# First weight pair of a sandwich block's gate and up products: fewer x splits beside it, down weights a pair later, the exponentials' tile kept

## The chip, the cores and the metric

The kernel runs on one core of a Trainium2 chip. The metric is the device time of one execution in microseconds, as the median of several runs. A profile of one execution shows each engine's instructions: TensorE (PE, with its weight loads PEld), VectorE (DVE), ScalarE (ACT), GpSimd (POOL), and the SP queue, which only issues DMAs here.

## What is computed

The input x has 2048 tokens of 1024 channels, everything in float32. The block is an attention part and a feed-forward part, each between two layer norms, each added to its input:

```python
def attn(x, Wqkv, bqkv, Wo, bo):
    qkv = x @ Wqkv + bqkv                        # one head, d = 256
    q, k, v = split(qkv)
    a = softmax(q @ k.T / sqrt(d))
    return (a @ v) @ Wo + bo
def ffn(x, W_gate, W_up, W_down):                # F = 2752
    return (silu(x @ W_gate.T) * (x @ W_up.T)) @ W_down.T
x = x + layernorm(attn(layernorm(x), Wqkv, bqkv, Wo, bo))
x = x + layernorm(ffn(layernorm(x), W_gate, W_up, W_down))
```

## The kernel before

**Products.** TensorE multiplies float32 numbers rounded to a shorter form (float32r). To keep precision each operand is kept as a high part and a low part, hi = round(a) and lo = a - hi. ScalarE makes the high part (a cast, L109 or L407), VectorE the low part (a subtraction, L110 or L408). One product of two blocks is then three matmuls, hi·hi, hi·lo and lo·hi (`mm3`, L144, and `mmc`, L602).

**Attention** goes by blocks of 128 queries, i = 0 to 15 (loop at L899). For a block the program computes scores (L244), the softmax into the tile `p_s` of 128 x 2048 (L253), four groups of transpositions of `p_s` that give the pieces of `pT` (`turn`, L263), the product with v (`attend`, L272: L276 and L277), the transposition of its result (`turn_o`, L282, with the copy L279 and the sum L280 before it) and the output projection (`proj`, L288). For the first 8 blocks the residual follows at once (`residual`, L299, and `xpose`, L342, which writes the transposed normalized rows to the DRAM tensors `xT_d`). For the last 8 blocks the projection only stores its rows in `at_d` (L297), and their residuals are done later, beside the gate and up products.

**Gate and up products** take two passes of 1024 tokens (s = 0, 1). In a pass there are 10 pairs of weight blocks (`gate_up`, L623). A pair multiplies 2 x 2 blocks by a scheme of Winograd's kind: seven products per weight matrix instead of eight, over sums of weight blocks (A11, A12, S1 to S4, A22) and sums of token blocks (B11, B21, B22, T1 to T4). Their order is A11·B11, A12·B21, S2·T2, S1·T1, S3·T3, A22·T4, S4·B22, each for gate and for up. With three matmuls for each of four blocks of channels, a product takes 12 matmuls of 128 x 512 (`prod`, L609, all of them on line L605). The four PSUM banks of a pass hold ag, au, cg and cu. ScalarE copies ag and au out (L637, L639 after A11·B11; L652, L654 after S2·T2; L661, L665 after S3·T3), VectorE adds (L618), ScalarE applies silu (L621), and the seven results are stored in `hd` (L634). The results lie in eight tiles `tmp` of 512 columns, which are halves of four tiles `xi`.

**The splits of x.** B11 and B21 lie in `xb`, T1 and T3 in `kx`, T2 in `qa` and `qb`, T4 and B22 in `a1`. During attention these tiles hold k, q and v, so the sums for the first pass are made early, stored in DRAM (`xs_d`, L417 and L418), and read back and split when a tile comes free. A `First` (L420) has a load into a float32 tile (L429) and a use (L407 and L408). They come in the list `order` (L939): the first four are loaded beside attention and used in its last round (L918); 4 to 9 are loaded and used from L946 on and in the first pair's jobs (`first`, `ahead`, `behind`).

**Beside a pair** of the first pass run three jobs, called from `background` (L629): after the A11 products, after the A12 products and after the S1 products. `ahead(p)` transposes the residual block of the pair before (`xpose`, L347 and L349), loads the attention rows and x of block 8 + p (L979, L980) and makes the sums of down weights of pair p (`down_weights`, L741: L744, three L618 and the four stores L749). `behind(p)` loads the next pair's down weights (`load_down`, L737) and does the residual of block 8 + p.

**Weights.** A feeder (L456) loads weight blocks (L511) and makes their sums (L529 to L532) and hi and lo parts whenever one of six slots is free; the slots are quarters of `a2` and halves of `wvo`, which attention uses until its end.

**Order on the engines.** A scheduler decides where an instruction stands in its engine's queue, by a model of time and the dependences between tiles. What is wrapped in `pin` (tc.keep_in_program_order) stays in the order of the program. Each queue then runs in order.

**Lines to follow:** `proj` L288 to L297, the tiles at L320 to L328, `tmp` in L626 and L698, the end of attention L943 to L958, the jobs L960 to L987, the loop over the pairs L989 to L996.

Of the kernel before, what the change touches and what calls it, by code (L numbers as in the profile page):

```python
# [8 lines left out]
F32 = mybir.dt.float32  # L9
# [6 lines left out]
P = 128  # L16
T = 2048
# [17 lines left out]
def block_kernel(ctx, tc, x, wqk, wv, bqk, bv, wo, bo, wgu, wlast, wd, out):  # L35
# [14 lines left out]
    def pool(name, side=None, **kw):  # L50
        return tc.alloc_tile_pool(name=name, bufs=1, side=side, reuse_waits="tile", **kw)

    def tl(p, shape, dt, name):
        return p.tile(shape, dt, tag=name, name=name, bufs=1)
# [231 lines left out]
        split(oTs[i % 2][:, :, 0, :], oTs[i % 2][:, :, 1, :], b.rearrange("p (d q) -> p d q", d=2))  # L286

    def proj(i):  # L288
        a = pair[i % 3][0] if i < EARLY else f4[i % 2]
        oT = oTs[i % 2]  # L290
        for h, b in ((1, bank[5]), (0, bank[7])):
            cols = slice(h * 512, h * 512 + 512)
            for d in range(2):
                mm3(b, (oT[:, d, 0, :], oT[:, d, 1, :]), (wo_s[:, d, 0, cols], wo_s[:, d, 1, cols]), d == 0, d == 1)
            nc.vector.scalar_tensor_tensor(a[:, cols], b, ys[i % 4][:, 13:14], bo_s[:, cols], ALU.mult, ALU.add)
        if i >= EARLY:
            nc.sync.dma_start(at_d[i], a)  # L297
# [22 lines left out]
    wpool = pool("w")  # L320
    wr = [tl(wpool, [P, C], F32, f"wr{i}") for i in range(2)]
    qb = tl(wpool, [P, 2, 2, 512], F32R, "qb")
    spool = pool("s")
    p_s = tl(spool, [P, T], F32, "p_s")
    oTs = [tl(spool, [P, 2, 2, P], F32R, f"oTs{i}") for i in range(2)]
    xe = tl(spool, [P, C], F32, "xe")
    xpool = pool("xb", side="right")
# [14 lines left out]
    def xpose(t, a, b, banks):  # L342
        for hf in range(2):
            o = banks[hf]
            for j in range(4):
                cb = 4 * hf + j
                nc.tensor.transpose(o[:, j * P : (j + 1) * P], a[:, cb * P : (cb + 1) * P], ident)  # L347
            s = b[:, hf * 512 : hf * 512 + 512]
            nc.scalar.copy(s, o)  # L349
            d = xT_d[t // TB][hf * 512 : hf * 512 + 512, (t % TB) * P : (t % TB + 1) * P]  # L350
            nc.sync.dma_start(d.rearrange("(j p) t -> p j t", p=P), s.rearrange("p (j t) -> p j t", j=4))
# [271 lines left out]
    def gate_up(s, p, wg, wu, bg, jobs):  # L623

        ag, au, cg, cu = bg
        g11, g12, g22, g21, u11, u12, u22 = tmp[0:7]  # L626
        job = list(jobs)

        def background():  # L629
            if job:  # L630
                job.pop(0)()

        def put(name, t):
            nc.sync.dma_start(hd[s][p][name], t)  # L634

        prod(ag, wg, "A11", "B11")
        nc.scalar.copy(g11, ag)  # L637
        prod(au, wu, "A11", "B11")
        nc.scalar.copy(u11, au)  # L639
        background()  # L640
        prod(cg, wg, "A12", "B21")
        wg.slot[0].done()
        add(g11, cg, g11)
        silu(g11, g11)
        prod(cu, wu, "A12", "B21")
        wu.slot[0].done()
        add(u11, cu, u11)
        add(g11, g11, u11, ALU.mult)
        put("A11", g11)
        background()  # L650
        prod(ag, wg, "S2", "T2", False)
        nc.scalar.copy(g12, ag)  # L652
        prod(au, wu, "S2", "T2", False)
        nc.scalar.copy(u12, au)  # L654
        prod(cg, wg, "S1", "T1")
        wg.slot[1].done()
        prod(cu, wu, "S1", "T1")
        wu.slot[1].done()
        background()
        prod(ag, wg, "S3", "T3", False)  # L660
        nc.scalar.copy(g22, ag)  # L661
        add(g22, cg, g22)
        silu(g22, g22)
        prod(au, wu, "S3", "T3", False)
        nc.scalar.copy(u22, au)  # L665
        add(u22, cu, u22)
        add(g22, g22, u22, ALU.mult)
        put("A22", g22)
        background()
        prod(ag, wg, "A22", "T4", False)  # L670
        wg.slot[3].done()
        silu(g21, ag)
        prod(au, wu, "A22", "T4", False)
        wu.slot[3].done()
        add(g21, au, g21, ALU.mult)
        put("A12", g21)
        prod(cg, wg, "S4", "B22", False)
        wg.slot[2].done()
        add(g12, cg, g12)
        silu(g12, g12)  # L680
        prod(cu, wu, "S4", "B22", False)
        wu.slot[2].done()
        add(u12, cu, u12)
        add(g12, g12, u12, ALU.mult)
        add(u22, g12, g22)
        add(u12, g11, g12, ALU.subtract)
        add(u11, u22, g11, ALU.subtract)
        add(g12, g21, u11, ALU.subtract)
        put("S1", u22)
        put("S3", u12)  # L690
        put("S2", u11)
        put("S4", g12)

    def gate_up_rest(s, wp, wu, bg):


        ap, au, cp, cu = bg
        g11, g12, g22, g21, u11, u12, u22 = tmp[0:7]  # L698
        prod(ap, wp, "A11", "B11")
        nc.scalar.copy(g11, ap)  # L700
        prod(au, wu, "A11", "B11")
        nc.scalar.copy(u12, au)
        prod(cp, wp, "A12", "B21")
        wp.slot[0].done()
        add(g11, cp, g11)
        silu(g11, g11)
        prod(cu, wu, "A11", "T1")
        prod(ap, wp, "S2", "T2", False)
        nc.scalar.copy(g12, ap)
        prod(au, wu, "A12", "B21", False)  # L710
        add(g11, au, g11, ALU.mult)
        nc.sync.dma_start(hr_d[s][0], g11)
        prod(cp, wp, "S1", "T1")
        wp.slot[1].done()
        prod(cu, wu, "A12", "B22", False)
        wu.one.done()
        add(u12, cu, u12)
        prod(ap, wp, "S3", "T3", False)
        nc.scalar.copy(g22, ap)
        add(u22[:FR, :], cp[FR : 2 * FR, :], g22[FR : 2 * FR, :])  # L720
        add(g22[:FR, :], cp[:FR, :], g22[:FR, :])
        silu(g22[:FR, :], g22[:FR, :])
        add(g22[:FR, :], g22[:FR, :], u22[:FR, :], ALU.mult)
        nc.sync.dma_start(hl_d[s][1], g22[:FR, :])
        prod(ap, wp, "A22", "T4", False)
        wp.slot[3].done()
        silu(g21[:FR, :], ap[:FR, :])
        add(g21[:FR, :], ap[FR : 2 * FR, :], g21[:FR, :], ALU.mult)
        nc.sync.dma_start(hl_d[s][0], g21[:FR, :])
        prod(cp, wp, "S4", "B22", False)  # L730
        wp.slot[2].done()
        add(g12, cp, g12)
        silu(g12, g12)
        add(g12, g12, u12, ALU.mult)
        nc.sync.dma_start(hr_d[s][1], g12)
# [206 lines left out]
                f.load(r)  # L942
    turn_o(NT - 1)  # L943
    proj(NT - 1)

    last = f4[2], f4[3], wr[1], bo_s  # L946
    for n in range(4, 8):
        order[n].load(last[n % 4])
    spool.release()
    xipool = pool("xi")  # L950
    xi = [tl(xipool, [P, C], F32, f"xi{i}") for i in range(4)]
    y = f4[0:4] + xi
    tmp = [xi[i // 2][:, (i % 2) * 512 : (i % 2) * 512 + 512] for i in range(8)]
    for n in range(2, 4):
# [2 lines left out]
        slots.free(flat(wvo[:, 2 * n : 2 * n + 2, :, :]))  # L957
    feed.pump()  # L958

    def late(p):  # L960
        return EARLY + p if 0 <= p < NT - EARLY else None

    def first(p):
        if p == 0:
            for n in range(4, 6):
                order[n].use()
                order[n + 4].load(last[n % 4])

    def ahead(p):

        if p == 0:
            for n in range(6, 10):
                order[n].use()
            raws2.free(wr[1])
            raws2.free(bo_s)
        if late(p - 1):
            xpose(late(p - 1), *f4[2:4], Y[0:2])
        if late(p):
            nc.sync.dma_start(f4[2], at_d[late(p)])  # L979
            nc.sync.dma_start(f4[3], x[late(p) * P : (late(p) + 1) * P, :])  # L980
        down_weights(p)

    def behind(p):
        if p + 1 < NPAIR:
            load_down(p + 1)
        if late(p):
            residual(late(p), *f4[2:4])  # L987

    load_down(0)  # L989
    for s in range(2):  # L990
        pairs, rest, dn = half[s]
        bg, other = (X, Y) if s == 0 else (Y, X)
        for p in range(NPAIR):
            jobs = [] if s else [lambda: first(p), lambda: ahead(p), lambda: behind(p)]
            gate_up(s, p, *pairs[p], bg, jobs)
        gate_up_rest(s, *rest, bg)  # L996

        def next_x(cb):
            r1, r2 = raws2.get(), raws2.get()
            build_x(2, cb, r1, r2)  # L1000
            raws2.free(r1)
            raws2.free(r2)

        if s == 0:
            run_down(s, dn, other, bg, 2 * TB * [None], [lambda cb=cb: next_x(cb) for cb in range(4)])
        else:
            xpool.release()
            x1pool = pool("x1", side="right")
            x1 = [tl(x1pool, [P, C], F32, f"x1_{k}") for k in range(2 * TB)]
            run_down(s, dn, other, bg, x1, [lambda k=k: nc.sync.dma_start(x1[k], x1_d[2 * TB + k]) for k in range(2 * TB)])  # L1010
# [39 lines left out]
```

## Time and profile before

| what | value |
|---|---|
| median of 3 runs (lowest, highest) | 1701.09 us (1698.03, 1702.44) |
| the profiled execution: its time, its span | 1700.9 us, 1699.1 us |
| mean granted TensorE clock | 0.996 |
| ScalarE, VectorE busy | 694.8 us (41%), 1100.3 us (65%) |
| chain that ended last: TensorE, VectorE, DMA | 92%, 4%, 2% |
| TensorE busy from 400 to 450 us | 46.68 us |
| TensorE busy from 450 to 500 us | 44.78 us |
| TensorE busy from 1100 to 1150 us | 48.67 us |

Times are in microseconds from the start of the span. A line of a timeline has the start, the duration, the engine, the line of the program, the operation with its output and input, and in brackets how long the engine sat idle before it and what ended that. The names of the tiles have lost their numbers, so `f` stands for f4[0] to f4[4] and f2_4. Matmuls overlap each other, so a matmul is drawn longer than the time by which it delays the next.

The chain of waits passes through the end of attention (about 437 us) into the first pair and the second one, which begins with its A11 products at 476.19 us.

### The profile page before, as it was taken

What the parts mean: (1) busy time and instruction counts of PE and PEld (TensorE: products, weight loads), DVE (VectorE), ACT (ScalarE), POOL (GpSimd) and SP (SyncE); (2) the same over time, 40 slices, a digit from 0 to 9 for tenths busy, and PEclk for the clock granted to TensorE, in tenths of its full rate; (3) what the DMA queues carried; (4) which work ended last, traced back from release to release, by engine and by line L of the source; (5) the groups of instructions that cost most, each with busy time, mean ns of one, the idle gap of its engine ahead of it and who ended that gap; (6) DMA issues with size and microseconds to landing.
All of it is one profiled execution on the core that took longest, in us unless ns stands there. A gap on an engine that the chain in (4) does not pass through costs nothing.

```text
span 1699.1 us, 21099 instructions
## 1 busy us (share of the span) xinstructions
PE 1669.2 (98%) x7764; PEld 1385.5 (82%) x7764; DVE 1100.3 (65%) x1682; ACT 694.8 (41%) x1039; POOL 91.3 (5%) x118
## 2 busy tenths in 40 slices
PE   8999999999899999999999999999999999999997
PEld 6888887888678888888888888788888888888886
DVE  8643667667787777776578457866555665455458
ACT  3222445544544444443365444433333333344343
POOL 1000000000011211110000000100000000000001
PEclk9999999999999999999999999999999999999999
DMA  6221123334676566665367666633332223566654
GB/s 214 81 81 38 38 75 121 101 118 169 218 243 209 200 215 212 217 220 183 122 204 252 215 191 198 210 106 113 130 111 100 93 94 124 209 221 192 195 189 158
DMA packets 131014, 271.00 MB, mean 159 GB/s; under 512 B 13280, under 2 KB 29792, under 8 KB 130912
## 3 DMA queue, kind: packets, MB, share of 16 engines
q1 hardware_dynamic: 128176, 262.72, 46.5%
q10 hardware_dynamic: 2736, 6.95, 1.2%
q8 instruction: 60, 0.98, 0.2%
q14 instruction: 42, 0.34, 0.1%
HBM read 185.73 MB, written 83.89 MB: 159 GB/s over the span
## 4 chain that ended last, share of the span: by engine, by line
PE 92%; DVE 4%; DMA 2%; ACT 1%; issue 1%; POOL 0%; SPq 0%; POOLq 0%; DVEq 0%; ACTq 0%
PE bank L605 69%; PE bank L146 4%; PE bank L147 4%; PE bank L148 4%; PE bank L276 3%; PE bank L277 2%; PE bank L206 2%; PE bank L268 1%; PE bank L207 1%; PE bank L347 1%; PE bank L139 1%; DVE a L110 1%; DVE small L116 0%; DMA f<-xT_d 0%; DVE wvo L110 0%
## 5 line engine op out<-in xcount | busy, mean ns | idle before, releaser
L605 PE MATMUL bank<-a 128*128 128x512 f32 x1164 | 274.2, 389 | 0.0
L605 PEld LDWEIGHTS bank<-a 128*128 128x128 f32 x1164 | 218.5, 188 | 45.3
L605 PE MATMUL bank<-xb,a 128*128 128x512 f32 x912 | 212.3, 389 | 0.1
L605 PEld LDWEIGHTS bank<-xb,a 128*128 128x128 f32 x912 | 171.1, 188 | 36.0 <-ACT xi L621 0.6
L618 DVE TENSOR_TENSOR xi<-bank,xi 128x512 f32<-128x512 f32 (+1 forms) x170 | 114.0, 682 | 115.0 <-PE bank L605 70.1
L110 DVE TENSOR_TENSOR a<-f2p,a 128x1024 fp32r<-128x1024 f32 (+2 forms) x133 | 134.6, 1012 | 58.0 <-ACT a L109 54.0
L109 ACT CAST a<-f2p 128x1024 fp32r<-128x1024 f32 (+2 forms) x133 | 117.5, 884 | 131.7 <-PE bank L605 107.2
L110 DVE TENSOR_TENSOR a<-f,a 128x1024 fp32r<-128x1024 f32 (+2 forms) x91 | 89.9, 988 | 106.5 <-ACT a L109 99.8
L605 PE MATMUL bank<-wvo 128*128 128x512 f32 x612 | 149.6, 389 | 0.0
L605 PE MATMUL bank<-kx,a 128*128 128x512 f32 x612 | 146.2, 389 | 0.0
L605 PE MATMUL bank<-a,a 128*128 128x512 f32 x588 | 140.2, 390 | 3.8 <-ACT xi L661 2.6
L605 PEld LDWEIGHTS bank<-kx,a 128*128 128x128 f32 x612 | 114.9, 188 | 23.8
L605 PEld LDWEIGHTS bank<-wvo 128*128 128x128 f32 x612 | 114.9, 188 | 23.9
L605 PEld LDWEIGHTS bank<-a,a 128*128 128x128 f32 x588 | 110.2, 188 | 27.5 <-ACT xi L661 3.0
L109 ACT CAST a<-f 128x1024 fp32r<-128x1024 f32 (+2 forms) x91 | 69.5, 764 | 141.6 <-PE bank L605 110.3
L605 PE MATMUL bank<-a,wvo 128*128 128x512 f32 x444 | 106.3, 389 | 0.0
L605 PE MATMUL bank<-kx,wvo 128*128 128x512 f32 x420 | 100.1, 389 | 0.0
L605 PEld LDWEIGHTS bank<-a,wvo 128*128 128x128 f32 x444 | 83.3, 188 | 17.3
L276 PE MATMUL bank<-a,a 128*128 128x512 f32 x256 | 94.6, 403 | 2.8 <-ACT f L349 2.0
L110 DVE TENSOR_TENSOR wvo<-f,wvo 128x1024 fp32r<-128x1024 f32 (+1 forms) x52 | 60.8, 1169 | 54.9 <-ACT wvo L109 53.8
L605 PEld LDWEIGHTS bank<-kx,wvo 128*128 128x128 f32 x420 | 78.8, 188 | 16.4
L618 DVE TENSOR_TENSOR xi<-xi,xi 128x512 f32<-128x512 f32 (+1 forms) x124 | 85.3, 688 | 5.6 <-ACT xi L621 1.5
(233 smaller groups left out, 2677.5 us busy)
## 6 DMA issues: line engine op xcount, KB each, us to landing
f2p<-wgu SPq DMA_DIRECT2D x41, 512.0 KB, 5.6
hd_S<-xi SPq DMA_DIRECT2D x80, 256.0 KB, 4.4
f<-x SPq DMA_DIRECT2D x30, 512.0 KB, 3.8
hd_A<-xi SPq DMA_DIRECT2D x60, 256.0 KB, 2.0
f<-wgu SPq DMA_DIRECT2D x22, 512.0 KB, 3.5
wr<-wgu SPq DMA_DIRECT2D x21, 512.0 KB, 5.9
f<-wd SPq DMA_DIRECT2D x20, 512.0 KB, 5.0
td_T<-f SPq DMA_DIRECT2D x40, 256.0 KB, 4.6
```

Of the source, the lines that this page charges most:

```text
L109: nc.scalar.copy(hi, src)
L110: (lo_engine or nc.vector).tensor_tensor(lo, src, f32(hi), ALU.subtract)
L139: nc.tensor.transpose(b[:, j * P : (j + 1) * P], t[:, cb * P : (cb + 1) * P], ident)
L146: nc.tensor.matmul(o, w[0], m[0], start=first, stop=False)
L147: nc.tensor.matmul(o, w[0], m[1], start=False, stop=False)
L148: nc.tensor.matmul(o, w[1], m[0], start=False, stop=last)
L206: nc.tensor.matmul(b, xg[:, c, 0, cols], wv_s[:, c, :, :].rearrange("p a f -> p (a f)"), start=(c == 0), stop=False)
L207: nc.tensor.matmul(b[:, D:], xg[:, c, 1, cols], wv_s[:, c, 0, :], start=False, stop=(c == 7))
L276: nc.tensor.matmul(b, p[:, k, 0, :], vt[:, k, :, :].rearrange("p h d -> p (h d)"), start=(k == 0), stop=False)
L277: nc.tensor.matmul(b[:, D:], p[:, k, 1, :], vt[:, k, 0, :], start=False, stop=(k == NKB - 1))
L605: one = nc.tensor.matmul(o, w[i], m[j], start=first and n == 0, stop=last and n == 2, skip_group_check=chained)
L618: nc.vector.tensor_tensor(o, a, b, op)
```

## The change

Five things change.

- The exponentials' tile `p_s` is kept: it is allocated in the pool `w`, not in `s`, which is released after attention. Its two halves become xi[0] and xi[1]. The results of a pair are named in another order over `tmp`, so that g11 and u11 lie in the first half of `p_s`, g12 and u12 in the second, g22 and u22 in xi[2] and g21 in xi[3].
- `proj` of the last block, 15, writes to `xe` and not to f4[1].
- The six x splits that remain at the end of attention (order 4 to 9) get six tiles to be loaded into in one go: f4[2], f4[3], wr[1], f4[1], f4[0], bo_s. Before, four were loaded, and two more after the first two had been used.
- In the first pair, `ahead` uses splits 4 and 5 and is called first, and `behind` uses 6 to 9.
- The residual blocks 8 to 15 come a pair later (block 8 + p - 1 beside pair p), and so do the down weights: `behind(p)` loads those of pair p, `ahead(p + 1)` makes their sums, and those of the last pair are made in a fourth job of the last pair.

```diff
     def proj(i):
-        a = pair[i % 3][0] if i < EARLY else f4[i % 2]
+        a = pair[i % 3][0] if i < EARLY else f4[i % 2] if i < NT - 1 else xe
...
     qb = tl(wpool, [P, 2, 2, 512], F32R, "qb")
+    p_s = tl(wpool, [P, T], F32, "p_s")
     spool = pool("s")
-    p_s = tl(spool, [P, T], F32, "p_s")
...
-        g11, g12, g22, g21, u11, u12, u22 = tmp[0:7]
+        g11, u11, g12, u12, g22, u22, g21 = tmp[0:7]
...
-    last = f4[2], f4[3], wr[1], bo_s
-    for n in range(4, 8):
-        order[n].load(last[n % 4])
+    last = f4[2], f4[3], wr[1], f4[1], f4[0], bo_s
+    for n in range(4, 10):
+        order[n].load(last[n - 4])
     spool.release()
     xipool = pool("xi")
-    xi = [tl(xipool, [P, C], F32, f"xi{i}") for i in range(4)]
+    xi = [p_s[:, 0:C], p_s[:, C:]] + [tl(xipool, [P, C], F32, f"xi{i}") for i in range(2)]
...
     def late(p):
-        return EARLY + p if 0 <= p < NT - EARLY else None
-
-    def first(p):
+        return EARLY + p - 1 if 1 <= p <= NT - EARLY else None
+
+    def ahead(p):
         if p == 0:
             for n in range(4, 6):
                 order[n].use()
-                order[n + 4].load(last[n % 4])
-
-    def ahead(p):
-
+            return
+        if late(p - 1):
+            xpose(late(p - 1), *f4[2:4], Y[0:2])
+        if late(p):
+            nc.sync.dma_start(f4[2], at_d[late(p)])
+            nc.sync.dma_start(f4[3], x[late(p) * P : (late(p) + 1) * P, :])
+        down_weights(p - 1)
+
+    def behind(p):
         if p == 0:
             for n in range(6, 10):
                 order[n].use()
             raws2.free(wr[1])
             raws2.free(bo_s)
-        if late(p - 1):
-            xpose(late(p - 1), *f4[2:4], Y[0:2])
-        if late(p):
-            nc.sync.dma_start(f4[2], at_d[late(p)])
-            nc.sync.dma_start(f4[3], x[late(p) * P : (late(p) + 1) * P, :])
-        down_weights(p)
-
-    def behind(p):
-        if p + 1 < NPAIR:
-            load_down(p + 1)
+        load_down(p)
         if late(p):
             residual(late(p), *f4[2:4])
 
-    load_down(0)
...
-            jobs = [] if s else [lambda: first(p), lambda: ahead(p), lambda: behind(p)]
+            jobs = [] if s else [lambda: None, lambda: ahead(p), lambda: behind(p)]
+            if s == 0 and p == 0:
+                jobs = [lambda: ahead(0), lambda: None, lambda: behind(0)]
+            if s == 0 and p == NPAIR - 1:
+                jobs.append(lambda: down_weights(NPAIR - 1))
```

More of the change, by code (lines that the diff above doesn't have):

```diff
@@ L697, in gate_up_rest @@
         ap, au, cp, cu = bg
-        g11, g12, g22, g21, u11, u12, u22 = tmp[0:7]
+        g11, u11, g12, u12, g22, u22, g21 = tmp[0:7]
         prod(ap, wp, "A11", "B11")
```

## The prediction

> **What bounds the kernel now.** I read the page's busy shares first, then TensorE's waits, then the timelines of TensorE, ScalarE and VectorE round the place that the change touches.
>
> ```profile
> PE 1669.2 (98%) x7764; PEld 1385.5 (82%) x7764; DVE 1100.3 (65%) x1682; ACT 694.8 (41%) x1039; POOL 91.3 (5%) x118
> ```
>
> TensorE (PE) is busy for 98% of the span, so an edit off TensorE can only win back idle time of TensorE. TensorE's waits, summed by who ended them (us in total, times, longest), show where that is:
>
> ```profile
> PE bank L605 <- ACT xi L637: 3.1, 2, 1.6
> PE bank L605 <- ACT xi L661: 2.6, 1, 2.6
> PE bank L285 <- DVE f L280: 1.3, 1, 1.3
> PE bank L605 <- ACT xi L639: 1.0, 1, 1.0
> ```
>
> All four belong to the first two weight pairs. TensorE's timeline (start, us, instruction, idle before it) puts them between 440 and 497 us:
>
> ```profile
> 440.31 0.44 PE L285 MATMUL bank<-ident,f 128*128 128x128 f32 x2 [1.32 <-DVE f L280]
> 441.21 0.50 PE L146 MATMUL bank<-wvo,oTs 128*128 128x512 f32 x1 [0.46 <-ACT oTs L109]
> 445.93 2.12 PE L605 MATMUL bank<-qa,a 128*128 128x512 f32 x8 [1.46 <-ACT xi L637]
> 465.17 5.74 PE L605 MATMUL bank<-a,a 128*128 128x512 f32 x24 [2.62 <-ACT xi L661]
> 470.75 5.60 PE L605 MATMUL bank<-a,wvo 128*128 128x512 f32 x24
> 476.19 11.04 PE L605 MATMUL bank<-xb,a 128*128 128x512 f32 x48
> 488.83 1.66 PE L605 MATMUL bank<-qa,a 128*128 128x512 f32 x6 [1.60 <-ACT xi L637]
> 494.43 1.03 PE L347 MATMUL bank<-ident,f 128*128 128x128 f32 x8
> 496.47 1.66 PE L605 MATMUL bank<-qa,a 128*128 128x512 f32 x6 [1.00 <-ACT xi L639]
> ```
>
> The six gaps sum to 1.32 + 0.46 + 1.46 + 2.62 + 1.60 + 1.00 = 8.46 us. A stream of matmuls costs 0.227 us each (470.75 to 476.19 is 24 of them), while a lone one is drawn 0.39 us long, so each gap costs 0.16 us more than it shows: 8.46 + 6 x 0.16 = 9.4 us, the ceiling of any gain here. From 500 to 1100 us, the table by 50 us has TensorE busy throughout.
>
> Why the gaps are there is in the queues of ScalarE and VectorE:
>
> ```profile
> 433.70 0.59 ACT L109 CAST a<-bank 128x512 fp32r<-128x512 f32 x1 [0.91 <-PE bank L268]
> 437.63 1.05 ACT L407 CAST a<-wr 128x1024 fp32r<-128x1024 f32 x1 [2.21 <-PE bank L277]
> 444.79 0.61 ACT L109 CAST a<-f 128x512 fp32r<-128x512 f32 x1
> 445.30 0.58 ACT L637 COPY xi<-bank 128x512 f32<-128x512 f32 x1
> 462.29 1.05 ACT L407 CAST a<-f 128x1024 fp32r<-128x1024 f32 x1 [3.56 <-DMA f<-xT_d]
> 464.54 0.58 ACT L661 COPY xi<-bank 128x512 f32<-128x512 f32 x1
> 446.75 0.68 DVE L110 TENSOR_TENSOR a<-f,a 128x512 fp32r<-128x512 f32 x1
> 450.38 1.22 DVE L408 TENSOR_TENSOR qb<-f,qb 128x1024 fp32r<-128x1024 f32 x1
> ```
>
> ScalarE takes its queue in order. The cast at 437.63 waits for the last attention matmul and holds up the copy behind the 1.32 us. L637 stands behind two weight casts (1.46). L661 stands behind casts of x splits still in flight (2.62).
>
> [...] at 98%, weight loads are busy 82%; I count gaps only. [...] the gaps end at evacuations (L637, L639, L661). [...] SP does so: it stores to `xs_d` at 424.09 and reads back at 427.19, after 2.7 us of waiting. [...]
>
> **The change part by part.** The built program's order tells what moves; durations are the trace's. Instruction counts hardly change (one VectorE instruction fewer), so no busy time is saved.
>
> 1. *Results in the exponentials' tile.* The first pair's result tiles g11 and u11 now lie in quarters of `p_s` already read. So L637, L639 and the table load move ahead of the last attention tile, and 20 products S1·T1 (L605 on kx) become free to run early: 2 inside attention(15), 18 between proj(14) and the transposition L285. 18 x 0.227 = 4.1 us cover the 1.32 gap (the chain L279, L280 takes about 1.7 us). Gone: 1.32 + 0.16 = 1.48. L637's gap goes too: 1.46 + 0.16 = 1.62. The 0.46 stays.
>
> New waits. (a) ScalarE now casts kx<-wr, kx<-xe, qb<-f, kx<-f ahead of the cast a<-bank on which attention(15) waits (433.70 before; TensorE reaches its matmul at 436.21, so there were 2 us of slack). L637, L639, table load and silu fill it to 431.6; the four casts take 0.96 each, but the last waits for data. The two loads of an x split into f4[1] now stand ahead on SP, so the write that wr's reload waits for ends about 1.4 us later (512 KB at some 370 GB/s), and the last of the six loads is issued near 430.3 instead of 429.5. Before, it took 5.9 us and landed at 435.4. Bounds: 434.8 (bytes over the rates seen) and 435.9 (before's spacing, shifted); I take 435.4. Then cast 435.4 to 436.4, a<-bank to 437.0: TensorE loses 0.78, and 0.27 more for the next weight cast (S1): 1.05. If the cover is gone, each us of lateness is a us. (b) The S2·T2 products lose their cover, the 20 kx products. Call T0 the end of L285 (440.76 before, about 445.0 after). VectorE's queue from there is full as before: the low parts of wvo, of the second S2 weight (446.75 before), then wvo again, then qb (450.38 before, now without the two L618 in front). They end at T0 + 6.68, + 7.74 and + 8.95. TensorE reaches the second S2 product's low part at T0 + 5.60 and waits 1.08; it reaches qb's low part at + 7.80 and waits 1.15. Bounds: 0 (were VectorE early) and 2.6. I take 2.23. Sum of part 1: -1.48 - 1.62 + 1.05 + 2.23 = +0.18 us. The early copies by themselves win nothing.
>
> 2. *The last x splits at once.* f4[1] and f4[0] are free since proj(15) writes to xe and the down weights come later, so all four a1 splits have landed when ScalarE reaches them (before: landing 7.7 us after issue, at 463.5). ScalarE can start them only after the copy L654 and two weight casts, near 458.9; four at 0.96 end at 462.7, and L661 at 463.3. TensorE ends S3·T3 at T0 + 17.6 = 462.7, 0.60 earlier. 2.62 + 0.16 falls to 0.60: -2.18. VectorE's low parts follow at 1.14 each, just ahead of TensorE, since the products are now ordered by block; the add before S4·B22 has only 0.2 us of slack. Bounds of what remains: 0 and 1.5.
>
> 3. *Down weights and residual out of the first pair.* L744, three L618, the statistics of L116 to L120: about 5.3 us of VectorE between 465 and 490, with ScalarE's L303 and L308 (1.2 each) and SP's at_d, td and x1_d transfers, go to the second pair and later. The last of it runs at the end of the tenth pair, where VectorE is 51% busy (800 to 850 us) and TensorE has work queued; if that cover were gone, 5 us of VectorE would show once. The second pair's L637 waited for VectorE's last L618 at 487.48. Now g11's last reader ends near 481.6 and the products reach bank 0 near 485: hidden with 3 us to spare. -1.60 - 0.16 = -1.76.
>
> 4. *No transposition beside the second pair.* L347 (8 matmuls) stood before L639's copy; ScalarE took it and L349 first. In the third pair and on, L639 precedes L349, and the trace shows no wait there. -1.00 - 0.16 = -1.16; the 8 transposes only move to the tenth pair. SP's loads of the second pair's weights move by a few us either way and are wanted more than 5 us after they land: no cost.
>
> Sum: 0.18 - 2.18 - 1.76 - 1.16 = -4.92 us. The profiled execution took 1700.9 us (span 1699.1); 1700.9 - 4.9 = 1696.0. The median of the runs shown is 1701.09, 0.2 above it, so 1696.1 us.
>
> **Rivals.**
> - *VectorE is early (greater gain).* If (b) falls away or the loads land at 434.8, the gain is 6 to 7.5 us: 1694. For it: VectorE has slack before 440. Against: from T0 its queue runs back to back.
> - *The late kx load takes it.* Loads land at 438 (the 7.7 us seen for the later ones): 2.6 us more of stall, 1698.9. For it: ScalarE's queue is in order, with attention behind. Against: fewer bytes are in flight at 430.
> - *The change does little but reorder*: that is part 1 as I work it out, and it would be the whole only if 2 and 3 failed: 1700 to 1701.
> - *Slower: the store of S2 becomes the bound in every pair.* L639 of each pair waits for the S2 store of the pair before (24.2 us of ScalarE waiting in eight pairs), and ends 1.9 us (third pair) or more before TensorE wants its bank. Should stores land over 1.9 us later with results packed in one tile, each of 17 pairs pays: 0.6 us beyond the point makes 17 x 0.6 = 10 us, 1706.3. Against: the order of stores on SP stays the same in every pair.
>
> **How the numbers follow.** Forecast 1696.1, own range 1694.3 to 1698.3: 0.58. Greater gain, 1692.5 to 1694.3: 0.20. Late load or little gain, 1698.3 to 1701: 0.15. Slower: 0.07. A change of under 0.3% (5.1 us) is about what a measurement of this kernel can't tell from none; that bound, 1696.0, cuts the forecast in two. Faster: 0.20 + 0.34 = 0.54; same: 0.24 + 0.15 = 0.39; slower 0.07. The range that leaves out 2 in 10 is 1692.8 to 1699.6.
>
> **What would show it.** Right: no gap before L285; S2·T2 with gaps of about 1 us ended by VectorE; the gap before A22·T4 under 1 us; none before the second pair's qa products; attention(15) waiting near 436 for ScalarE. Wrong: a gap over 2 us near 436, gaps in pairs 2 and on ended by L639, or a new gap before S4·B22.

## The result and the profile after

The changed kernel takes 1695.7 us in the median of twelve runs (1695.3 to 1698.5). The kernel before, run beside it, takes 1699.56 (1697.95 to 1703.6). The ratio is 0.9977, with a 95% interval of 0.9968 to 0.9986: 3.9 us faster (2.4 to 5.4). On a second chip it came to 0.9986 (0.9980 to 0.9993), 1696.3 us and 2.4 us faster. So the forecast of 1696.1 us holds. The forecast gain of 4.9 us does not quite: the kernel before ran 1.5 us faster beside it than the 1701.09 on which the sum was built. Both gains lie under the bound of 0.3%.

On the page, TensorE is busy for as many microseconds as before, in a shorter span (1693.5 us, the execution itself 1695.4 us):

```profile
PE 1669.1 (99%) x7764; PEld 1385.6 (82%) x7764; DVE 1098.7 (65%) x1682; ACT 695.1 (41%) x1039; POOL 91.2 (5%) x118
```

TensorE's timeline from 430 to 505 us has five gaps in place of six:

```profile
437.68 0.51 PE L276 MATMUL bank<-a,a 128*128 128x512 f32 x1 [1.39 <-ACT a L109]
446.31 0.50 PE L146 MATMUL bank<-wvo,oTs 128*128 128x512 f32 x1 [0.46 <-ACT oTs L109]
452.54 1.19 PE L605 MATMUL bank<-qa,a 128*128 128x512 f32 x4 [0.98 <-DVE a L110]
454.81 2.56 PE L605 MATMUL bank<-qb,a 128*128 128x512 f32 x10 [0.84 <-DVE qb L408]
464.66 5.73 PE L605 MATMUL bank<-a,a 128*128 128x512 f32 x24 [0.94 <-ACT xi L661]
```

The gaps before L285 and of the first L637 are gone, and so are both gaps of the second pair. In their place stand the waits that the prediction named: 1.39 us ahead of attention(15), and 0.98 and 0.84 us in S2·T2. L661's gap is down from 2.62 to 0.94. The sum of the gaps falls from 8.46 to 4.61.

ScalarE's timeline shows what ends them:

```profile
434.75 1.05 ACT L407 CAST qb<-f 128x1024 fp32r<-128x1024 f32 x1
436.10 1.05 ACT L407 CAST kx<-f 128x1024 fp32r<-128x1024 f32 x1 [0.29 <-DMA f<-xs_d]
437.05 0.58 ACT L109 CAST a<-bank 128x512 fp32r<-128x512 f32 x1
...
463.08 1.04 ACT L407 CAST a<-bo_s 128x1024 fp32r<-128x1024 f32 x1
464.03 0.57 ACT L661 COPY xi<-bank 128x512 f32<-128x512 f32 x1
```

The cast of the last exponentials (437.05) stands behind a cast that waits for its load (436.10). L661 follows the casts of a1 at once; none of these waits for data any more.

**One execution is not enough here.** There are three profiles of each kernel. Three things vary between executions of the same program: how late the last x splits land, whether TensorE's granted clock falls to 0.50 for 3.4 us (below), and how long the start of the second pass takes. Stage A runs from TensorE's transposition L285 at 424.4 us to the kx,wvo products of the tenth pair (near 810), stage C from the next such products (near 1083) to the first qa,wvo products of the second pass (near 1115). The 272.0 to 272.5 us between them, and the rest after C, hardly change.

| kernel, profile | A, us | of it lost to a halved clock | L661's gap | C, us |
|---|---|---|---|---|
| before, 1 | 388.53 | - | 2.62 | 33.70 |
| before, 2 | 386.07 | - | 0.92 | 33.62 |
| before, 3 | 389.48 | 1.6 | 2.15 | 31.73 |
| changed, 1 | 384.72 | - | 0.94 | 32.04 |
| changed, 2 | 385.61 | - | 1.74 | 31.74 |
| changed, 3 | 386.09 | 1.6 | 0.46 | 33.53 |

In the means, A falls by 2.6 us (388.03 to 385.47). That is the change. C takes either about 31.9 or about 33.6 us with either kernel, so it belongs to the execution. Where it is long, TensorE waits 1.2 us for L665's copy, and on SP's queue a store (`out<-wr`, near 1071 us) is followed by the reload of its tile after 5.6 to 5.8 us, where C is short after 4.9 to 5.0 (SP's timeline, three profiles each). That the slower store makes L665 late is not shown, and why it is slower in some executions stays open. The first pair of profiles, taken alone, would have credited the change with 1.7 us of that.

### The profile page after: what moved, and what is told of

Its sections match the earlier page's. It is cut to its first block, busy times and chain, and to the rows that moved or that the text cites. A ratio compares the mean times of both kernels' runs of the same rounds, so it can differ in the third digit from the quotient of the medians.

```text
span 1693.5 us, 21093 instructions
## 1 busy us (share of the span) xinstructions
PE 1669.1 (99%) x7764; PEld 1385.6 (82%) x7764; DVE 1098.7 (65%) x1682; ACT 695.1 (41%) x1039; POOL 91.2 (5%) x118
## 4 chain that ended last, share of the span: by engine, by line
PE 94%; DVE 2%; issue 1%; DMA 1%; ACT 1%; POOL 0%; POOLq 0%; DVEq 0%; SPq 0%; ACTq 0%
PE bank L605 71%; PE bank L147 4%; PE bank L146 4%; PE bank L148 4%; PE bank L276 3%; PE bank L277 2%; PE bank L206 2%; PE bank L268 1%; PE bank L207 1%; PE bank L347 1%; PE bank L139 1%; DVE small L116 1%; PE bank L784 0%; PE bank L785 0%; DMA f<-x 0%
## 5 line engine op out<-in xcount | busy, mean ns | idle before, releaser
L618 DVE TENSOR_TENSOR p_s<-bank,p_s 128x512 f32<-128x512 f32 x96 | 65.1, 682 | 78.4 <-PE bank L605 43.2
L121 POOL TENSOR_TENSOR small<-small,mhalf 128x1 f32<-128x1 f32 x48 | 38.0, 792 | 702.6 <-DVE small L120 670.7
```

What stands on the lines that cost most here:

```text
L121: nc.gpsimd.tensor_tensor(s[:, 15:16], s[:, 14:15], mhalf, ALU.pow)
L618: nc.vector.tensor_tensor(o, a, b, op)
```

## The experiments

Each ratio is to runs of the kernel before on the same chip.

**Part 1 alone.** The kernel before with the results in the exponentials' tile:

```diff
+    p_s = tl(wpool, [P, T], F32, "p_s")
     spool = pool("s")
-    p_s = tl(spool, [P, T], F32, "p_s")
...
-        g11, g12, g22, g21, u11, u12, u22 = tmp[0:7]
+        g11, u11, g12, u12, g22, u22, g21 = tmp[0:7]
...
-    xi = [tl(xipool, [P, C], F32, f"xi{i}") for i in range(4)]
+    xi = [p_s[:, 0:C], p_s[:, C:]] + [tl(xipool, [P, C], F32, f"xi{i}") for i in range(2)]
```

> Part 1 alone: the kernel before with the results of a pair in the exponentials' tile; loads, down weights and residual stay as before. My theory (early copies win nothing by themselves): the gaps before L285 (1.32 us) and of the first L637 (1.46 us) go, but TensorE waits for ScalarE's cast ahead of attention(15) (0.5 to 1.4 us) and for VectorE in S2*T2 (about 2 us); L661's gap of 2.6 us and the second pair's gaps of L637 and L639 stay. Time within 1 us of before: 1698.9 to 1700.6. Rival (the early copies are what wins): the two gaps go and nothing comes for them, 3.1 us faster, about 1696.5.

Measured: 1704.14 us, ratio 1.0022 (1.0014 to 1.0030), so 3.7 us slower. TensorE's timeline has eight gaps; two of them:

```profile
451.74 1.19 PE L605 MATMUL bank<-qa,a 128*128 128x512 f32 x4 [0.99 <-DVE a L110]
...
465.90 7.35 PE L605 MATMUL bank<-a,a 128*128 128x512 f32 x24 [2.00 <-ACT xi L661]
```

The waits in S2·T2 (0.99 and 0.84) and ahead of attention(15) (0.57) take the place of the gaps won, as my theory had it, and the rival falls. It is slower than I expected, and the one profile shows two reasons. L652 (0.69) now waits behind the cast a<-bo_s, whose load is late. And the 24 products at 465.90 take 7.35 us where 5.74 is usual. The table of this stretch by single us shows why; the third last column is the clock granted to TensorE:

```profile
465.00:466.00 1.00, 0.10 (x1) 0.10 (x1) 1.00 (x3) 1.00 (x3) 0.00 (x0) 1.00 0.00 0
466.00:467.00 1.00, 1.00 (x3) 0.80 (x4) 1.00 (x2) 0.33 (x1) 0.00 (x0) 0.57 0.70 188
467.00:468.00 1.00, 1.00 (x3) 0.72 (x3) 1.00 (x3) 0.00 (x0) 0.00 (x0) 0.50 0.86 332
468.00:469.00 1.00, 1.00 (x4) 0.79 (x3) 1.00 (x3) 0.62 (x1) 0.00 (x0) 0.50 0.89 102
469.00:470.00 1.00, 1.00 (x5) 0.82 (x4) 1.00 (x3) 0.56 (x1) 0.00 (x0) 0.73 0.85 233
```

After the gap TensorE runs at half clock for 3.4 us, and 7.35 - 5.74 = 1.6 us are lost that no gap shows.

**Without part 1.** The changed kernel with the same three edits taken back:

> The changed kernel without part 1: results in four tiles that wait for the end of attention, as before; loads at once, down weights and residual a pair later. My theory: parts 2 to 4 give the whole gain and part 1 costs about 1.1 us, so this one is 4.5 to 5 us faster than before, about 1694.8, and faster than the changed kernel by about 1 us; gaps of 1.3 us before L285 and 1.5 us of L637 are back, none before attention(15) and none in S2*T2. Rival (part 1 is needed for the gain): it loses the two gaps of 3.1 us and ends near 1698 or later.

Measured: 1696.7 us, ratio 0.9981 (0.9974 to 0.9987), 3.2 us faster than before; the changed kernel's own two ratios (0.9977, 0.9986) lie on either side. So the rival falls: the gain does not need part 1. My 1 us over the changed kernel did not show in the times either. The gap before L285 did not come back to 1.3 us but is 0.27: the cast a<-wr that held it up has moved with the last splits from `ahead` to `behind`, which belongs to part 3, so this gap would have gone without part 1. L637's gap, though, grows to 2.39. ScalarE's timeline has one more weight cast ahead of this copy than before, wvo<-f2p, about 0.95 us:

```profile
444.84 1.04 ACT L109 CAST wvo<-f2p 128x1024 fp32r<-128x1024 f32 x1
445.79 0.57 ACT L637 COPY xi<-bank 128x512 f32<-128x512 f32 x1
```

Again the products behind the gap are slow (12 take 4.61 us, where 2.9 is usual):

```profile
446.42 4.61 PE L605 MATMUL bank<-qa,a 128*128 128x512 f32 x12 [2.39 <-ACT xi L637]
464.96 5.74 PE L605 MATMUL bank<-a,a 128*128 128x512 f32 x24 [0.31 <-ACT xi L661]
```

Stage A takes 385.15 us in this profile, 1.7 of them lost to the halved clock. Without that loss it would be some 1.5 us shorter than the changed kernel's mean, so a cost of part 1 of that size may be hidden here; with one profile this is an estimate.

**Parts 3 and 4 alone.** The kernel before with `late`, `ahead`, `behind` and the jobs as changed, and with its own four and two loads:

```diff
-        return EARLY + p if 0 <= p < NT - EARLY else None
+        return EARLY + p - 1 if 1 <= p <= NT - EARLY else None
...
-        down_weights(p)
+        down_weights(p - 1)
...
-        if p + 1 < NPAIR:
-            load_down(p + 1)
+        load_down(p)
```

> Parts 3 and 4 alone: down weights and residual a pair later, results and loads as before. My theory: the gaps before the second pair's products on qa (1.60 by L637, 1.00 by L639) go, those of the first pair (1.32, 1.46, 2.62) stay: 2.9 us faster, about 1696.7, and nothing is given back in the last pair. Rival (the work shows up again where it is moved to): a new gap in the tenth pair or in the rest of the first pass takes it back, 1698.5 to 1700.

Measured: 1697.77 us, ratio 0.9984 (0.9978 to 0.9991), 2.7 us faster (1.5 to 3.7). Both gaps of the second pair are gone, and no new one follows up to the second pass; the rival falls. This is most of the whole change. The gap before L285 is 0.27 here too, as without part 1. L661's gap is 3.06 us, with half clock behind it.

**Part 2 undone.** The changed kernel with four loads, and two more after the first two have been used:

```diff
-    last = f4[2], f4[3], wr[1], f4[1], f4[0], bo_s
-    for n in range(4, 10):
-        order[n].load(last[n - 4])
+    last = f4[2], f4[3], wr[1], bo_s
+    for n in range(4, 8):
+        order[n].load(last[n % 4])
...
                 order[n].use()
+                order[n + 4].load(last[n % 4])
```

> The changed kernel with part 2 undone: four of the last x splits are loaded, and two more when the first two have been used, into the same tiles. My theory: L661 waits for the late data again, gap 2.3 to 2.8 us in place of 0.94, so 1.3 to 1.9 us slower than the changed kernel, 1697.0 to 1697.6, unless the wait ahead of attention(15) shrinks too because fewer loads stand ahead. Rival (ScalarE's casts alone hold L661): the gap stays at about 1 us and the time at 1695.7.

Measured: 1697.97 us, ratio 0.9989 (0.9982 to 0.9995). That is 0.5 to 2 us behind the changed kernel, with intervals that overlap. L661's gap is 0.50 us and not 2.3, so my theory of the gap fails and the rival's figure for it is nearer, though the time is not the rival's 1695.7. As its runs scatter (1695.6 to 1701.7), I profiled it again:

> The changed kernel with part 2 undone, a second profile: its first had L661's gap at 0.50 us and was near the lower end of its runs (1695.9, median 1698.0). If part 2 takes away a wait whose length varies, this profile has a gap of 0.5 to 3 us ended by f<-xT_d, and where it exceeds 2 us the clock may halve behind it; if part 2 does nothing, the gap stays near 0.5 us and the scatter comes from the start of the second pass (31.7 to 33.7 us).

L661's gap was 1.19, and none of the casts of a1 waited for an x split; TensorE waited 2.08 us ahead of attention(15). With part 1 in place TensorE comes to L661 some 2 us later (in the first profile at 463.9, against 461.6 with parts 3 and 4 alone), and the late data have landed by then. With part 1 in place the gap is 0.50 and 1.19 without part 2, and 0.94, 1.74 and 0.46 with it. Without part 1 it is 3.06 us without part 2 and 0.31 with it, but that does not isolate part 2 either: in the second of these profiles TensorE, held up by L637 and the slow products, came to L661 at 464.65, 3 us later than the 461.61 of the first, and the copy itself was no earlier (464.33 against 464.04). The times of the two, 1696.7 and 1697.77 us, have ratios whose intervals overlap.

**The changed kernel again**, beside the next two:

> The changed kernel once more, on the chip and beside the runs of the two variants that follow: 1695.7, gaps of about 1.4 us before attention(15), 1.0 and 0.8 us in S2*T2 and 0.9 us of L661, none of 2 us or more after 50 us, so the granted clock stays at 1.00 from there to the last product. At the start of the second pass: if what was seen there belongs to the kernel, no gap of L665; if it belongs to the single execution, 0 to 1.2 us.

Measured: 1696.33 us, ratio 0.9986 (0.9980 to 0.9993), gaps of 1.47, 0.98, 0.84 and 1.74. In this execution L661 was late behind weights (a cast waited 1.14 us for `f<-wgu`), not behind x splits.

**Attention's cast kept ahead of the late casts.** I kept the split in `turn(15, 3)` in program order, and moved the use of the first four splits ahead of it:

```diff
+        if i == NT - 1:
+            for f in order[:4]:
+                f.use()
-        turn(i, 3)
+        turn(i, 3, pin if i == NT - 1 else lambda m: m)
```

> The changed kernel with the split of the last exponentials (turn(15, 3)) kept ahead of the casts qb<-f and kx<-f on ScalarE; nothing else moves. My theory (the stall ahead of attention(15) is ScalarE holding that cast behind a cast that waits for a load): the 1.39 us gap goes, with 0.2 to 0.5 us behind it, the gaps in S2*T2 stay: 1.5 to 1.9 us faster than the changed kernel, about 1694.0. Rival (TensorE is only handed on to the next wait: the weight casts or VectorE): the gap moves and the time stays at 1695.5.

Measured: 1700.75 us, ratio 1.0008 (1.0000 to 1.0017), some 4 us slower than the changed kernel. The edit did not do what I meant. SP's order followed it: six half-tile loads, where three stood, went ahead of the store of wr to `xs_d`. The store was issued at 427.1 (424.3 in the changed kernel), wr's reload at 432.4 (429.0). ScalarE:

```profile
436.05 1.05 ACT L409 CAST kx<-wr 128x1024 fp32r<-128x1024 f32 x1 [3.84 <-DMA wr<-xs_d]
437.00 1.04 ACT L409 CAST kx<-xe 128x1024 fp32r<-128x1024 f32 x1
437.94 0.58 ACT L271 CAST a<-bank 128x512 fp32r<-128x512 f32 x1
```

TensorE waits 1.96 us for this cast and 0.91 for VectorE behind it. As a test of the rival it says nothing. But it lengthens the suspected wait and TensorE pays: attention's cast behind casts of late x splits is what TensorE waits for.

**Both new waits taken away.** The last two splits of the first pair, qb and the last block of kx, stand ahead of `turn_o(15)` and `proj(15)` in the program:

```diff
+    last = f4[2], f4[3], wr[1], f4[1], f4[0], bo_s
+    for n in range(4, 6):
+        order[n].load(last[n - 4])
+        order[n].use()
     turn_o(NT - 1)
     proj(NT - 1)
-    last = f4[2], f4[3], wr[1], f4[1], f4[0], bo_s
-    for n in range(4, 10):
+    for n in range(6, 10):
         order[n].load(last[n - 4])
...
         if p == 0:
-            for n in range(4, 6):
-                order[n].use()
             return
```

> The changed kernel with the last two splits of the first pair (qb and the last block of kx) loaded and used ahead of turn_o(15) and proj(15) in the program: their casts come after L279 on ScalarE, their low parts in VectorE's idle time near 443 us, ahead of the low parts of wvo and S2. My theory: the wait ahead of attention(15) goes (1.39), the waits in S2*T2 go (0.98 and 0.84), six products on kx fill the 0.46 us gap before proj(15): with 0.16 us for each, 3.6 to 4.3 us faster than the changed kernel, 1691.4 to 1692.1. Rival (VectorE and ScalarE are only late elsewhere): a wait for the low part of the second S2 weight, or L654 and the casts of a1 now in another order, takes half of it back, 1693.5 to 1694.5.

> The variant with the last two splits of the first pair early, once more, with more timed runs: five runs gave 1692.26, with a profile of 1695.5 that began 1.4 us late and took 34.5 us at the start of the second pass. Expected 1692 to 1693.5, 3 to 4 us faster than the changed kernel; gaps: 0.7 in attention(15) by VectorE, 1.5 of L654 behind three casts of a1. Rival (the five runs were a lucky draw): 1694.5 or more.

Measured: 1692.26 us, ratio 0.9959 (0.9945 to 0.9973), and on another chip 1693.49, 0.9966 (0.9952 to 0.9979), five runs each. This version beats both kernels: the kernel before by 5.8 to 7.0 us, the changed one by 4.1 us on the chip where both ran. Stage A takes 380.95 and 381.06 us, against 385.47 in the mean of the changed kernel: 4.5 us less (3.9 less without the halved clock), so the expected 3.6 to 4.3 are there in this stage. The times themselves lie 0.2 and 1.4 us above the expected 1691.4 to 1692.1, and the second is at the rival's edge. The casts of qb and kx now follow L279 on ScalarE, and their low parts fill VectorE's idle time; in VectorE's timeline of the second of these runs:

```profile
441.79 0.74 DVE L295 SCALAR_TENSOR_TENSOR f<-bank,ys,bo_s 128x512 f32<-128x512 f32 x1
442.45 1.22 DVE L408 TENSOR_TENSOR qb<-f,qb 128x1024 fp32r<-128x1024 f32 x1
443.58 1.22 DVE L408 TENSOR_TENSOR kx<-f,kx 128x1024 fp32r<-128x1024 f32 x1
```

Two gaps remain in TensorE's:

```profile
438.84 0.38 PE L277 MATMUL bank<-a,a 128*128 128x256 f32 x1 [0.78 <-DVE a L110]
459.33 3.02 PE L605 MATMUL bank<-kx,wvo 128*128 128x512 f32 x12 [1.52 <-ACT p_s L654]
```

The second is new: L654 stands behind three casts of a1. It is part of what the rival expected.

**The scatter.** Two more profiles of the kernel before and a third of the changed one give the table above:

> The kernel before, a second profile. If a gap of TensorE of 2 us or more can halve the granted clock behind it (seen at gaps of 2.0, 2.4 and 3.1 us in the three variants, not at the 2.62 us in the first profile of before), then this profile either shows 3.4 us at half clock after L661's gap and is about 1.7 us longer in that stage, or shows none. If the clock has nothing to do with the gap, no stretch under 1.00 is found behind it in either.

> The kernel before, a third profile, for the scatter: L661's gap was 2.62 and 0.92 us in the first two, the stage at the start of the second pass 33.7 and 33.6 us long. If the late x splits make the gap, it follows the landing of the last f<-xT_d and lies anywhere from 0.9 to 3.1 us; the start of the second pass, if it belongs to the kernel, takes 33.6 us again.

> The changed kernel, a third profile, for the scatter: L661's gap 0.9 to 1.8 us, waited for by weights (f<-wgu) and not by x splits; no gap of 2 us after 50 us; the start of the second pass, if it belongs to the kernel, takes 31.7 to 32.0 us again (before: 33.6).

The second profile of before had L661's gap at 0.92, with no half clock, and the gap before L285 at 0.62:

```profile
439.92 0.44 PE L285 MATMUL bank<-ident,f 128*128 128x128 f32 x2 [0.62 <-DVE f L280]
463.07 5.74 PE L605 MATMUL bank<-a,a 128*128 128x512 f32 x24 [0.92 <-ACT xi L661]
```

The third, whose last x split was waited for until 462.89, had it at 2.15 with 24 products in 7.36 us behind it:

```profile
464.48 7.36 PE L605 MATMUL bank<-a,a 128*128 128x512 f32 x24 [2.15 <-ACT xi L661]
```

The changed kernel's third profile had no gap of 2 us and was halved all the same, after two short ones in S2·T2 (10 products in 4.16 us, 2.56 in the first profile). C took 31.73 us with the kernel before and 33.53 with the changed one: it does not belong to the kernel.

## Why the prediction was right in its time, and where its sum was wrong

- **Parts 3 and 4, right.** Predicted -1.76 and -1.16. The gaps of L637 and L639 in the second pair are 1.59 to 1.60 and 1.00 in all three profiles of before, and 0 in all of the changed kernel. Alone they give 2.7 us, where 2.9 were predicted, but that includes the gap before L285, which fell with them to 0.27 and which the prediction had left out of these parts. The tenth pair hides what was moved there, as assumed.
- **Part 1, right that it wins nothing, with terms that were off.** "The early copies by themselves win nothing" is borne out: alone it is 3.7 us slower, and with parts 2 to 4 it makes no difference that the times show. In its terms: (b), VectorE in S2·T2, was predicted at 2.23 and is 0.98 + 0.84 + 2 x 0.16 = 2.14. (a), ScalarE's cast behind the late load, was under-sized: the gap was predicted at 0.78 and is 1.39 to 1.59. L637, L639, the table load (1.28 us in both traces) and silu filled ScalarE to 431.9, near the forecast 431.6. The step that failed is the landing of the last kx load. I took it at 435.4, when it had landed before, although its issue had moved back by 0.8 us; my bounds were 434.8 and 435.9. The cast behind it starts at 436.10 to 436.36. The store of wr with two more loads of 256 KB ahead of it was followed by its reload after 4.7 us (424.34 to 429.04), against 3.1 before, and the last of the six loads was issued near 430.8 and not 430.3. The 1.32 before L285 was credited to part 1 though part 3 takes most of it, and it was one execution's value: 1.32, 0.62 and 1.15 in the three profiles of before. In the second and third, the cast at L407 that holds L285 up waited for the load `wr<-xT_d` (1.50 and 2.04 us) and not for the last attention matmul. With the means of the gaps, part 1's sum is nearer +1.0 than +0.18 us.
- **Part 2, wrong in size.** Predicted -2.18, from 2.78 to 0.60. The wait for x splits is gone, as forecast. But 2.62 us was one execution's value, of three that gave 2.62, 0.92 and 2.15, mean 1.90. What remains was predicted at 0.60 and is 0.94, 1.74 and 0.46, mean 1.05. I had the casts of a1 start near 458.9; they started at 460.23, 461.10 and 461.63. In the first, 0.84 of the 1.3 us is L285, which ended at 445.84 and not 445.0 and holds TensorE back as much; in the second a weight cast waited for its load; in the third TensorE itself was slow. So the term is about -0.9 in the means. Even that is not shown to be part 2's: TensorE now comes later to L661 (463.72 in the first profile, 462.55 before), and the run with part 2 undone, with part 1 in place, has gaps no longer than these. What part 2 does take away is the waiting for the landing itself.
- **The rivals.** S2's store did not become the bound: L639 ends no gap in any pair. The late kx load is half true: 436.1 to 436.4, not 438. VectorE was not early.
- **The sum.** 0.18 - 2.18 - 1.76 - 1.16 = -4.92 was forecast; the runs give -2.4 and -3.9, the mean of stage A -2.6. Of the 2.3 us that stage A misses, the means of the gaps put 1.3 to part 2, 0.6 to (a) and 0.3 to the gap before L285. That the time came out to 0.4 us is in part luck: the kernel before was itself some 1.5 us under the median that I started from.

**What I did not consider: the clock.** My "ceiling of any gain" counted each gap at its length and 0.16 us. A gap can cost 1.6 us more (7.35 - 5.74 in part 1 alone). Between 35 and 1680 us the 14 traces show five halvings of the granted clock. Worked out from the clock column, each lasted 3.40 to 3.42 us. Halvings followed gaps of 2.00, 2.15, 2.39 and 3.06 us, and in the changed kernel's third profile 0.99 and 0.85 us with 1.4 us of products between them:

```profile
454.00:455.00 1.00, 0.21 (x1) 0.00 (x0) 1.00 (x2) 0.00 (x0) 0.00 (x0) 1.00 1.00 313
455.00:456.00 1.00, 0.94 (x2) 0.83 (x3) 1.00 (x2) 0.00 (x0) 0.00 (x0) 0.55 1.09 336
456.00:457.00 1.00, 1.00 (x4) 0.73 (x3) 0.14 (x1) 0.00 (x0) 0.00 (x0) 0.50 0.93 363
```

Gaps of 2.62 us (the first profile of before) and 2.08 us (the second profile with part 2 undone) were followed by no halving, so the length of the gap alone does not tell. What does was not shown, and no run varied it by itself.

## What to carry to other kernels

When the bound is a few gaps of one engine, profile the kernel before several times: a gap that waits for a load is a different number in each execution (L661's was 2.62, 0.92 and 2.15 us), and only gaps set by queue order (1.60 and 1.00 here, three times of three) can be subtracted as they stand. Moving work early gains only as far as the work behind it on each in-order engine moves too; the changed kernel gained another 4 us once the last splits were moved too (1692 to 1693 us). Whether that needs the early copies was not tried. Beside each idle gap look at the granted clock just behind it, since a gap may cost 1.6 us more, as 2.15 us did in the third profile of before.

## What the runs showed of the hardware that I had not expected

- TensorE's granted clock was 0.50 for 3.4 us behind single gaps of 2.00 to 3.06 us and behind a pair of 0.99 and 0.85 us, but not behind gaps of 2.62 and 2.08 us. 24 products then took 7.35 us instead of 5.74.
- With two more 256 KB loads ahead of a 512 KB store on its queue, the reload of its tile went 4.7 us after the store's issue, instead of 3.1.
- The start of the second pass takes 31.7 to 33.7 us with the same code, in the three profiles each of two kernels; in the variants it took up to 34.5. Its cause is open.
